# The tiles of an attention's close in a pool opened first: a two-layer graph attention kernel

## The chip, the cores and the metric

The kernel runs on one core of a Trainium2 chip. The metric is the device time of one execution in microseconds (us). A core has five engines, each with its own instruction stream in a fixed order: TensorE (PE in the profile; its weight loads are PEld), VectorE (DVE), ScalarE (ACT), GpSimd (POOL) and SyncE (SP), which here issues most of the DMAs. They wait for one another through semaphores.

## The reference, cut to what matters

4096 rows of 256 numbers go through three graph attentions with four heads each, an iterated feed-forward net (FFN) after the first, and a routed mixture of experts (MoE) after the third:

```python
def gat(x, adj, W, a):                       # 4 heads, D = 64
    h = einsum('nf,hfd->hnd', x, W)
    e = leaky_relu(f1[:, :, None] + f2[:, None, :], 0.2)   # f1, f2: h against a
    att = softmax(where(adj > 0, e, NEG))
    return elu(einsum('hnm,hmd->hnd', att, h))

x = x + gat(layernorm(x), adj, L0)           # first attention
x = x + ffn(layernorm(x))                    # 30 steps
h1 = gat(layernorm(x), adj, W1, a1)          # second attention
x = x + gat(h1, adj, W2, a2)                 # third attention
x = x + moe(layernorm(x))                    # top 2 of 6 experts
```

The third attention takes all its rows from the second one's result.

## The kernel before, in words

The function `attention` is called three times, with tags g0, g1 and g2. Each call has two stages.

**Preparation.** The 4096 rows are taken in eight groups of 512. For a group, `load` brings its rows into one of four slots of the tile `ring`, `columns` transposes them on PE (L114, into the PSUM tile `tp`) and ACT copies them to `xT` (L276). `products` multiplies by the weights (PE, L302, into two PSUM tiles `ph`), DVE copies the score columns out to `fs` (L320), ACT the rest to `hc` (L322). In the first group `greatest` finds a maximum (L283 to L292). Then come the exponentials `bd` (L329), the row `rt` that is stored to memory as `fd`, the scaled values `v` (L370) and, by `upper` and `lower`, the split tile `vals` (L377, L382), 66,560 bytes of each partition. `vals` stays for the second stage.

**Main loop.** 128 units follow one another, one for each of four chunks of 1024 rows, four heads and eight steps of 512 columns. ACT and DVE form a step mask `st` from the broadcast scores `f1b` (L461, L459), DVE joins it with the adjacency mask `m` (L567) and makes its complement `below` (L573), PE multiplies both by `vals` into the PSUM tile `acc` (L519). The order of DVE and ACT is written out by hand here; elsewhere a planner sets the order of each engine's stream, and it takes the waits for memory into account.

**The close.** When the eight steps of a chunk and head are done, ACT takes `lo` from `acc` (L468), DVE adds to `u` (L472) and works on `u` in five more operations (L482 to L494), ACT takes an exponential `e` (L497), and `finish` combines them (L623 or L625, then L626) and stores `e` (L627): to `h1d` in the second attention, and in the third to `x3d`, after adding the tile `old` that was loaded from `x2d`. A close is spread over the next unit's steps. Only the last one of an attention has nothing to hide behind.

The tiles of the on-chip memory come from pools. A pool takes the next free bytes when it is opened, in the manner of a stack, and gives them back when its scope ends; a tile that is put over an older one waits for everything that still reads or writes the older one. Within `attention` the pools were opened in this order: `lay` (r, nf2, hs), `vals`, `mask`, `f`, `steps`; then, for the preparation alone, `prep` and `pw` (xs, fs, mb, xT, hc, gm, bd, rt, v), which are closed at its end; and then `end` (u, lo, z, e, and old) and `work` (below). So `end` and `work` lie where the preparation had been, and since the three calls have the same pools, the third call's preparation lies where the second call's `end` is.

After the third attention the MoE opens its own pools from the same place on: bT, acc (32 KB, the running result), the expert weights ew0 to ew2, then the router's tiles. Its function `route` normalises rows (DVE L101 to L111, POOL's power L106, DVE L1108 and L1111), transposes (PE L1119), multiplies twice (L1098, ACT's relu L1100, L1128), and sorts rows to experts; POOL makes index constants (L1043 to L1072); SP loads the experts' weights (L1296). The main loop over tiles of 128 gathered rows follows (gather L1312, weight copies L1343).

Of the kernel before, what the change touches and what calls it, by code (L numbers as in the profile page):

```python
# [46 lines left out]
def gnn_ffn_kernel(ctx: ExitStack, tc: tile.TileContext, a: dict, out: bass.AP):  # L47
# [113 lines left out]
    def attention(tag, src, norm, w, front, chunks, first, ends, following, side={}):  # L161
# [7 lines left out]
        with ExitStack() as scope:  # L169
            lay = scope.enter_context(tc.tile_pool(name=f"{tag}_lay", bufs=1))  # L170
            r = lay.tile([P, NT, H], F32, name="r")
            nf2 = lay.tile([P, NT, H], F32, name="nf2")
            hs = lay.tile([P, 1, H, DV], F32, name="hs")
            vals = scope.enter_context(tc.tile_pool(name=f"{tag}_vals", bufs=1)).tile(
                [P, NT, H, 2, 2, DV], F16, name="vals"
            )
# [258 lines left out]
                )  # L435
                nc.gpsimd.memset(hs[:, 0, :, D : D + 1], TINY * N)  # L436

            end = scope.enter_context(tc.tile_pool(name=f"{tag}_end", bufs=1))
            if first:
                mask.append(scope.enter_context(tc.tile_pool(name=f"{tag}_mask1", bufs=4)))  # L440
            work = scope.enter_context(tc.tile_pool(name=f"{tag}_work", bufs=2))
            ps_o = scope.enter_context(tc.tile_pool(name=f"{tag}_pso", bufs=1, space=PSUM))
# [294 lines left out]
    first = ctx.enter_context(tc.tile_pool(name="f_first", bufs=4))  # L737
# [49 lines left out]
    def front(prep, small_ps):  # L787
# [22 lines left out]
        1: [(measure, 3), (init, 0), (init, 1), (rate, 2), (rate, 3)],  # L810
    }
    attention(
        "g0",
        x,
# [183 lines left out]
    for n in range(2):  # L998
        attention(
            f"g{n + 1}",  # L1000
            h1d if n else x2d,
            not n,
            layers[n + 1][0],
            None if n else centre_weights,
            [8, 8, 8, 8],
            False,
            to_rows(x3d, x2d) if n else to_rows(h1d),
            [NG // 2, x3d, runs_of] if n else [2, h1d],
            {} if n else side,
        )  # L1010
# [7 lines left out]
    with ExitStack() as scope:  # L1018
# [261 lines left out]
        with tc.tile_pool(name="r_ps", bufs=1, space=PSUM) as psum, tc.tile_pool(  # L1280
            name="r_pst", bufs=4, space=PSUM
# [186 lines left out]
```

## Time and profile before

| what | us |
|---|---|
| median of 3 runs | 2985.34 |
| lowest and highest | 2984.63, 2988.94 |
| the profiled execution | 2984.29 |
| its span, first to last instruction | 2982.6 |
| last `acc` matmul of the second attention ends | 2111.2 |
| first `below` of the third attention | 2178.72 |
| last `acc` matmul of the third attention ends | 2661.4 |
| first gather of the MoE | 2712.5 |

The page gives busy times, the granted clock of PE and the groups of instructions; the timeline gives single instructions with their start in us from the start of the span, their duration, and in brackets the time that the engine had been idle before and what released it. All times in this document from one kernel's trace are of one execution.

### The profile page before, as it was taken

To read this page: it belongs to the slowest core of one execution; us is meant where nothing else is said; L and a number is where in the kernel's file an instruction comes from. 1 tells how busy PE (TensorE), PEld (TensorE's weight loads), DVE (VectorE), ACT (ScalarE), POOL (GpSimd) and SP (SyncE) were. 2 spreads that over 40 slices of the span, in tenths; PEclk is the share of its full clock that TensorE was granted. 3 is DMA by queue.
4 is the path that set the end of the run, shared out by engine and by line. 5 is a ranking of instruction groups with operands and counts; after the bars stand their busy time and mean duration, and the time that the engine had idled before them with its cause. 6 is when DMAs were issued, how large, how long until landed. Compare 5 with 4: busy or idle time off the path is not lost. (4 is left out here: it accounts for less than half of the span.)

```text
span 2982.6 us, 82658 instructions
## 1 busy us (share of the span) xinstructions
PE 2801.3 (94%) x33923; PEld 2561.3 (86%) x33923; DVE 2740.8 (92%) x5769; ACT 2465.6 (83%) x3125; POOL 1153.7 (39%) x1084
## 2 busy tenths in 40 slices
PE   7899999979999999999998999999889999986996
PEld 5899999958888888888887999999789999975996
DVE  7999999999999999999998899999689999986775
ACT  6799999888888888888877999999699999963342
POOL 3000000079999999999982000000200000014663
PEclk9999999989999999999999999999999999998998
DMA  9999885153333333333353022120302132123253
GB/s 288 274 256 250 224 248 140 27 128 68 68 68 68 68 68 68 68 68 68 68 115 111 27 97 74 47 87 27 107 20 94 52 108 80 52 90 133 80 173 135
DMA packets 484450, 320.07 MB, mean 107 GB/s; under 512 B 416589, under 2 KB 445418, under 8 KB 477930
## 3 DMA queue, kind: packets, MB, share of 16 engines
q1 hardware_dynamic: 474034, 290.27, 36.7%
q0 software_dynamic: 7104, 19.41, 2.1%
q8 instruction: 268, 4.39, 0.6%
q10 hardware_dynamic: 2936, 5.11, 0.5%
q14 instruction: 108, 0.88, 0.1%
HBM read 183.00 MB, written 52.04 MB: 79 GB/s over the span
## 5 line engine op out<-in xcount | busy, mean ns | idle before, releaser
L519 PE MATMUL acc<-vals,st 128*128 128x130 f16 x12288 | 1430.7, 218 | 37.7 <-DVE u L472 30.2
L519 PE MATMUL acc<-vals,below 128*128 128x130 f16 x12288 | 1430.3, 221 | 12.9 <-DVE below L573 12.2
L461 ACT ACTIVATE st<-f1b,nf 128x1024 int8<-128x1024 f32 x1265 | 1334.5, 1140 | 30.8 <-PE acc L519 23.0
L519 PEld LDWEIGHTS <-below 128*128 128x128 fp8e4 x12288 | 1175.0, 96 | 53.4 <-issue 46.8
L519 PEld LDWEIGHTS <-st 128*128 128x128 fp8e4 x12288 | 1207.1, 98 | 8.9 <-DVE st L567 7.0
L935 PE MATMUL po<-wT,zT 128*128 128x256 f32 x1920 | 575.4, 382 | 6.9 <-ACT zT L922 3.7
L938 PE MATMUL po<-w,zT 128*128 128x256 f16 x3840 | 577.3, 273 | 0.4 <-DMA zT<-z 0.4
L906 POOL TENSOR_TENSOR th<-th,y 128x1024 f32<-128x1024 f32 x232 | 548.6, 2365 | 14.8 <-DVE z_st L915 0.4
L938 PEld LDWEIGHTS <-zT 128*128 128x128 f16 x3840 | 375.8, 98 | 161.3 <-DMA zT<-z 1.1
L573 DVE TENSOR_TENSOR below<-m,st 128x1024 int32<-128x1024 int32 x384 | 469.9, 1224 | 32.6 <-DVE st L567 0.9
L567 DVE TENSOR_TENSOR st<-st,m 128x1024 int32<-128x1024 int32 x384 | 467.1, 1216 | 0.2
L875 DVE SCALAR_TENSOR_TENSOR y<-po,z_rs,bias 128x256 f32<-128x256 f32 x928 | 384.3, 476 | 2.2 <-PE tp L867 0.7
L915 DVE BATCH_NORM_STATS2 z_st<-z 128x6 f32<-128x256 f32 x960 | 335.4, 411 | 0.0
L935 PEld LDWEIGHTS po<-wT,zT 128*128 128x128 f32 x1920 | 290.9, 192 | 16.4 <-ACT zT L922 4.5
L891 ACT ACTIVATE z<-th 128x1024 f32<-128x1024 f32 x240 | 251.8, 1049 | 17.4 <-POOL th L906 16.7
L106 POOL TENSOR_TENSOR ln_rstd<-ln_rstd,mhalf 128x4 f32<-128x4 f32 x24 | 31.0, 1293 | 578.0 <-ACT acc L1121 491.7
L926 POOL TENSOR_TENSOR z_rs<-z_rs,mhalf 128x4 f32<-128x4 f32 x240 | 245.0, 1021 | 3.1 <-ACT z_rs L925 3.1
L905 ACT ACTIVATE th<-y 128x1024 f32<-128x1024 f32 x232 | 241.9, 1043 | 0.0
L922 ACT COPY zT<-tp 128x512 f32<-128x512 f32 x240 | 140.2, 584 | 91.0 <-PE tp L867 89.8
L459 DVE TENSOR_SCALAR st<-f1b,nf 128x1024 int8<-128x1024 f32 x271 | 201.0, 742 | 7.5 <-PE acc L519 7.5
L758 POOL TENSOR_TENSOR x_rs<-x_rs,mhalf 128x4 f32<-128x4 f32 x8 | 9.4, 1174 | 501.8 <-ACT x_rs L757 501.8
L436 POOL MEMSET hs<- 128x4 f32 x3 | 0.3, 101 | 492.5 <-DVE u L489 492.5
(263 smaller groups left out, 3133.6 us busy)
## 6 DMA issues: line engine op xcount, KB each, us to landing
ring<-in_adj_dram SPq DMA_DIRECT2D x64, 1024.0 KB
m<-edges SPq DMA_DIRECT2D x32, 1024.0 KB
f1b<-fd SPq DMA_DIRECT2D x48, 512.0 KB
edges<-m SPq DMA_DIRECT2D x16, 1024.0 KB
y<-yd SPq DMA_DIRECT2D x16, 512.0 KB
ew<-in_L_ffn_expert_w_dram SPq DMA_DIRECT2D x18, 256.0 KB
t<-in_x_dram SPq DMA_DIRECT2D x8, 512.0 KB
old<-in_x_dram SPq DMA_DIRECT2D x16, 256.0 KB
```

Source lines behind the costliest of these rows:

```text
L461: nc.scalar.activation(out, f1, AF.Sign, bias=f2, scale=-1.0)
L519: nc.tensor.matmul(acc[:, i, cols], masked[part][:, at_i // TR, s, rows], v[:, cols], start=(j == 0 and part == 0), stop=(j == NT - 1 and ...
L567: nc.vector.tensor_tensor(above, above, whole, OP.bitwise_and)
L573: nc.vector.tensor_tensor(below, whole, above, OP.bitwise_xor)
L875: nc.vector.scalar_tensor_tensor(t[:, r, :] if end else y[:, g * G + r, :], po[:, r, :], rstd[:, r : r + 1], t[:, r, :] if end else bias, ...
L891: ins = nc.scalar.activation(z, th.pop(u), AF.Silu, scale=0.01)
L905: nc.scalar.activation(th[at], was, AF.Tanh, scale=0.01)
L906: ins = (nc.gpsimd if at else nc.vector).tensor_tensor(th[at], th[at], was, OP.add)
L915: nc.vector.bn_stats(st[:, r, :], z[:, r, :])
L926: nc.gpsimd.tensor_tensor(rs[u], rs[u], mhalf, OP.pow)
L935: nc.tensor.matmul(po[:, r, :], src[:, r * P : (r + 1) * P], wT, start=True, stop=False)
L938: nc.tensor.matmul(po[:, r, :], src16[:, part * G + r, :], w16[:, other, :], start=False, stop=(part == 1 and other == 1),)
```

## The change

In the second and third attention the pool `end` is opened right after `lay`, ahead of `vals`; it is no longer opened after the preparation. In the first attention it stays where it was. No operation is added or removed.

```diff
             hs = lay.tile([P, 1, H, DV], F32, name="hs")
+            end = None if first else scope.enter_context(tc.tile_pool(name=f"{tag}_end", bufs=1))
             vals = scope.enter_context(tc.tile_pool(name=f"{tag}_vals", bufs=1)).tile(
                 [P, NT, H, 2, 2, DV], F16, name="vals"
             )
...
-            end = scope.enter_context(tc.tile_pool(name=f"{tag}_end", bufs=1))
             if first:
+                end = scope.enter_context(tc.tile_pool(name=f"{tag}_end", bufs=1))
                 mask.append(scope.enter_context(tc.tile_pool(name=f"{tag}_mask1", bufs=4)))
             work = scope.enter_context(tc.tile_pool(name=f"{tag}_work", bufs=2))
```

From the added line on, the line numbers of the kernel after are one higher than here (L303 for L302, and so on).

## The prediction

> **What bounds the kernel now.** I read the page first for which engine sets the pace, then the timeline around the place where the second attention ends and the third is prepared, then the one-microsecond stretches there with TensorE's granted clock, and last the timeline where the third attention ends, since the same pool lies under the router's tiles.
>
> ```profile
> PE 2801.3 (94%) x33923; PEld 2561.3 (86%) x33923; DVE 2740.8 (92%) x5769; ACT 2465.6 (83%) x3125; POOL 1153.7 (39%) x1084
> ```
>
> TensorE (PE) is busy 94% of the span, so time is to be had only where it stands still. The page's chain of work that ended last begins at 2633 us and doesn't reach the seam at 2111 us. The timeline there (start, duration, engine, line, form, then idle time before it and its releaser), first PE, then VectorE (DVE), ScalarE (ACT) and the DMA queue of SyncE (SP):
>
> ```profile
> 2112.61 1.09 PE L114 MATMUL tp<-ident,ring 128*128 128x128 f32 x8 [1.43 <-DVE u L472]
> 2122.43 5.99 PE L302 MATMUL ph<-g_w,xT 128*128 128x264 f32 x16 [8.73 <-ACT xT L276]
> ...
> 2116.88 0.69 DVE L626 SCALAR_TENSOR_TENSOR e<-e,u 128x512 f32<-128x512 f32 x1
> 2126.36 0.17 DVE L320 COPY fs<-ph 128x16 f32<-128x16 f32 x1 [8.79 <-PE ph L302]
> 2128.45 0.17 DVE L320 COPY fs<-ph 128x16 f32<-128x16 f32 x1 [1.92 <-PE ph L302]
> ...
> 2115.75 0.63 ACT L497 ACTIVATE e<-u 128x512 f32<-128x512 f32 x1 [3.93 <-DVE u L494]
> 2121.69 0.60 ACT L276 ACTIVATE xT<-tp 128x512 f32<-128x512 f32 x1 [5.31 <-DMA h1d<-e]
> ...
> 2117.60 0.37 SPq L627 DMA_DIRECT2D h1d<-e  x1
> ```
>
> The third attention's first rows are loaded and transposed by 2113.70. Their copy into xT nevertheless starts at 2121.69, released by the landing of the close's last store, 4.09 us after its issue. PE stands for 8.73 us. That isn't a need of the data: rows 0 to 511 have nothing to do with the last chunk's result. It is the memory. In the built program the close's tiles (u, lo, z, e) lie at bytes 171104 to 181536 of each partition, and xT's two buffers at 173376 to 181568.
>
> The clock column (PE, its weight loads, DVE, ACT, POOL busy; then the clock) for four of these microseconds:
>
> ```profile
> 2114.00:2115.00 1.00, 0.00 (x0) 0.00 (x0) 0.92 (x3) 0.00 (x0) 0.10 (x1) 1.00 0.95 401
> 2116.00:2117.00 1.00, 0.00 (x0) 0.00 (x0) 0.55 (x2) 0.38 (x1) 0.00 (x0) 0.80 1.03 437
> 2124.00:2125.00 1.00, 1.00 (x4) 0.80 (x3) 0.00 (x0) 0.00 (x0) 0.00 (x0) 0.50 0.00 0
> 2127.00:2128.00 1.00, 1.00 (x6) 0.87 (x5) 0.00 (x0) 0.15 (x1) 0.00 (x0) 1.00 0.00 0
> ```
>
> The standstill costs twice: at 2116.8 the clock falls to half, and the 16 matmuls that follow take 5.99 us, where the same 16 take 3.83 later (2155.81).
>
> [...] 0.50 from 2117, 1.00 again 4 us into the matmuls. [...] reusing e's bytes costs the store's 4.09 us and not its 0.37 us of issue. [...] in the trace, DVE slows beside POOL's work there: four scalings L1111 took 1.38 us at 2669.67 and 2.14 at 2680.20 beside POOL's casts.
>
> **The change part by part.** It adds and removes no instruction, byte or load; it moves tiles. In the second and third attention the close's tiles go to 47200 to 57632, under vals. The preparation then starts at 181536, where the below tiles lie (181536 to 193824).
>
> 1. Start of the second attention: vals and the masks move 10,432 bytes up over other FFN tiles. Wait for wait, its instructions wait for the same ones as before. Cost 0; were the cover gone, PE's last FFN matmul would already hold the same tiles.
>
> 2. Seam from second to third, the gain. The first xT now waits only for the transposes and DVE's last sum; ACT takes both halves ahead of e. Step by step: transposes end 2113.70; xT 2113.73 to 2114.99 (two halves took 1.26 us at 2121.69), so e at 2115.75 isn't delayed. PE starts 0.74 us after xT's start, as before: 2114.47. It then has stood 0.77 us, so I take the warm 3.83 us: the second ph ends at 2118.3. DVE is now the one to be late: in its order the close still stands ahead of fs, until 2117.57. So the first fs is at 2117.6 (its ph, five eighths of the matmuls in, is there at 2116.9) and the second at 2118.35, against 2128.45: **10.1 us less**. With a cold clock (5.99 us) the second ph ends at 2120.46: 8.0 us less. I take warm: the clock held for 5.6 us after the last attention matmul (2111.2), and now new matmuls come after 3.3. What follows is one chain (maximum, mb, bd, v, vals), which moves along: from 2131 to 2178 us ACT is busy 43.7 and DVE 41.7 of 47 us, and both move as one, so nothing there takes the gain up. External times that don't move: the next-layer masks fill the DMA queues until 2120, first used at 2152.89; the row load of group 4 was issued at 2113.73 and is needed near 2130; groups 6 and 7 read the last chunk, landed 2121.69, and their load would come at 2122.5, after it. On SP's queue the last store stands between the loads of groups 4 and 5; its time is unchanged and group 5's slot frees at about 2119.5. Cost 0 each.
>
> 3. Entry to the router, where three waits change:
>
> ```profile
> 2666.74 1.04 POOL L106 TENSOR_TENSOR ln_rstd<-ln_rstd,mhalf 128x4 f32<-128x4 f32 x1 [491.71 <-ACT acc L1121]
> 2673.91 0.21 POOL L1043 IOTA along_i<- 128x37 int32 x1
> 2678.53 1.05 POOL L106 TENSOR_TENSOR ln_rstd<-ln_rstd,mhalf 128x4 f32<-128x4 f32 x1
> ...
> 2665.54 2.42 SPq L1296 DMA_DIRECT2D ew<-in_L_ffn_expert_w_dram  x5
> 2669.04 0.37 SPq L627 DMA_DIRECT2D x3d<-e  x1
> ...
> 2690.00:2695.00 5.00, 0.00 (x0) 0.00 (x0) 4.20 (x19) 0.93 (x3) 0.00 (x0) 0.85 1.01 402
> 2695.00:2700.00 5.00, 0.38 (x4) 0.16 (x3) 4.27 (x21) 0.61 (x1) 0.00 (x0) 0.50 0.07 28
> ```
>
> POOL's constants needed the close's bytes; now they need only the last matmuls (2661.3) and are ordered ahead of the first power L106. They hold it for about 6.6 us (2673.91 to 2681.55 less one power of 1.05), to 2667.9 instead of 2666.74; its user on DVE, nmr, came at 2669.22 and hides that, but casts beside the close's two-input sums may add up to 1.5. The fourth power, queued behind the constants until 2678.53, is free at about 2677. The router's acc now lies over e (45248 to 78016), and bT, which the first relu needs, also waits for the last x3d store: issued 2669.04, landing at 2673.1 by the 4.09 us above. bT stands in DVE's order ahead of the second n, which so starts up to 1.2 us late; three acc of 1.07 us on ACT stand before the first relu, which comes at 2676.4 to 2677.1 instead of 2676.22. PE is nearly full from 2670.13 to 2689.95 and follows: logits done between 0.1 earlier and 0.5 later. The five expert loads ahead of that store now come after it: all 18 (256 KB each) start at about 2673.5 instead of 2665.5. At the 400 GB/s of these rows 4.7 MB take 12 us, so they land near 2692 with the others between them, ahead of the first use at 2700.7. Unseen in the trace is how the constants run beside the close: bounds 2 us gained (fourth power) and 2.5 lost (first power, bT, relu in a row). I take **0.5 us lost**.
>
> Sum: -10.1 + 0.5 = -9.6 us. The profiled execution took 2984.29 us (span 2982.6), so 2974.7; the median of the three runs, 2985.34, lies 1.05 above it, so I say **2975.7**.
>
> **The rivals.** *Cold clock.* The transposes may not count as activity[...]. Against it: clock 1.00 up to 2116. Gives -8.0 + 0.5: 2977.8. *The router gains*: -10.1 - 2.0 gives 2973.2; for it speaks nmr at 2679.61, which waited for that fourth power, against it that PE is full there. *No change*: another wait at the seam takes over, so that xT or ph still comes with the close's store. The wait lists speak against it; 2985.3. *Slower*: the expert loads, pushed behind the store, land late, and the loop's first weight copies (2700.7 on ACT) wait. Each microsecond past 2700.7 costs one; from 2710.3 on the gain is eaten, which needs 4.7 MB in 37 us, 128 GB/s instead of 400. At 100 GB/s they'd land at 2720.5: 19.8 lost, 2995.5.
>
> **How the numbers follow.** Forecast 0.66, cold clock 0.15, router gains 0.10, no change 0.05, slower 0.04. The range runs from 2972.0 (router's bound of 2 and 1.2 of run-to-run spread) to 2980.5 (cold clock, router's loss of 2.5, and 0.7 of spread). 0.2%, 6 us, is about what a measurement of this kernel can tell from no change; cold clock with the worst router gives only -5.5 and counts as no change. Faster 0.88, same 0.08, slower 0.04.
>
> **What would show it.** Right: ACT's first xT of the third attention near 2114 with PE tp as releaser, the matmuls L302 after under 1 us of idle time in about 3.8 us, fs following e within 1 us, the third attention's first below 10 us earlier. Step 3 right: the stretch from the last acc matmul to the first gather, 51.1 us now (2661.4 to 2712.5), within 2.5 of that. Wrong: PE idle over 3 us before L302, or w<-ew released by a DMA.

## The result, and the profile after

The kernel after takes 2977.12 us (median of 7 runs, 2973.72 to 2981.28), the kernel before, also in 7 runs, 2987.28 us (2982.51 to 2988.94): a ratio of 0.9971, 95% interval 0.9962 to 0.998. That is 8.7 us less by the ratio, between 6.0 and 11.4. Run again later, where both took 11 to 13 us longer, the same two kernels stood at 0.9956 [0.9942, 0.9969], 13.2 us less. The profiled execution after took 2978.01 us, its span 2976.1, against 2982.6 before. The page's first row after:

```profile
PE 2800.0 (94%) x33923; PEld 2562.3 (86%) x33923; DVE 2740.5 (92%) x5769; ACT 2465.1 (83%) x3125; POOL 1157.6 (39%) x1084
```

PE is busy 1.3 us less, DVE and ACT as long as before: the time came out of standstills, and of the matmuls that ran at half clock.

The seam from the second to the third attention, timeline of the kernel after, PE first, then DVE, ACT and SP's queue:

```profile
2113.65 1.09 PE L114 MATMUL tp<-ident,ring 128*128 128x128 f32 x8 [1.43 <-DVE u L473]
2115.52 3.83 PE L303 MATMUL ph<-g_w,xT 128*128 128x264 f32 x16 [0.78 <-ACT xT L277]
...
2117.93 0.69 DVE L627 SCALAR_TENSOR_TENSOR e<-e,u 128x512 f32<-128x512 f32 x1
2118.53 0.17 DVE L321 COPY fs<-ph 128x16 f32<-128x16 f32 x1
2119.39 0.18 DVE L321 COPY fs<-ph 128x16 f32<-128x16 f32 x1 [0.69 <-PE ph L303]
...
2114.78 0.60 ACT L277 ACTIVATE xT<-tp 128x512 f32<-128x512 f32 x1 [1.92 <-PE tp L114]
2116.80 0.63 ACT L498 ACTIVATE e<-u 128x512 f32<-128x512 f32 x1 [0.75 <-DVE u L495]
...
2118.65 0.37 SPq L628 DMA_DIRECT2D h1d<-e  x1
```

Read from the transposes' start (2113.65), since executions of one and the same kernel reach this place up to 2.4 us apart. ACT takes xT 1.13 us after it, released by the transposes and no longer by the store, which is issued only 3.9 us later. PE stands 0.78 us instead of 8.73, and its 16 matmuls take 3.83 us instead of 5.99. The second fs comes 5.74 us after the transposes' start; before it was 15.84. This is 10.1 us less. DVE's tail of the close now ends last: the first fs follows e<-e,u without a gap.

The entry to the router, first one line of DVE in the kernel before, then the timeline of the kernel after (POOL, DVE, SP's queue, ACT, POOL):

```profile
2663.10 0.68 DVE L482 TENSOR_TENSOR u<-u,r 128x520 f32<-128x520 f32 x1
...
2652.68 0.17 POOL L1044 IOTA along_i<- 128x37 int32 x1 [486.60 <-PE acc L520]
2660.40 1.47 POOL L106 TENSOR_TENSOR ln_rstd<-ln_rstd,mhalf 128x4 f32<-128x4 f32 x1
...
2654.24 1.05 DVE L483 TENSOR_TENSOR u<-u,r 128x520 f32<-128x520 f32 x1
2661.91 0.16 DVE L1109 SCALAR_TENSOR_TENSOR nmr<-ln_mv,ln_rstd 128x4 f32<-128x4 f32 x1 [0.77 <-POOL ln_rstd L106]
2662.39 1.38 DVE L1112 TENSOR_SCALAR n<-ring,ln_rstd,nmr 128x256 f32<-128x256 f32 x4
...
2667.46 11.04 SPq L1297 DMA_DIRECT2D ew<-in_L_ffn_expert_w_dram  x16
...
2692.53 1.66 ACT L1344 COPY w<-ew 128x512 f32 x3 [6.16 <-DMA ring<-x3d]
...
2704.31 1.61 POOL L1313 DMA_INDIRECT gx<-nd,source  x1 [0.25 <-DVE ln_mv L103]
```

POOL runs the index constants from 2652.68 on, beside the close, and gets to its first power only at 2660.40; nmr waits for it. I measure from the start of the last close's u<-u,r, which the constants hardly move (from the second lo of the close, ahead of it, the loss is 0.68). In the kernel before it was at 2663.10: the first scaled n came 6.57 us later (2669.67) and the first gather 49.41 (2712.51). After, these are 8.15 and 50.07. The router lost 0.66 us.

In the two profiles of the kernel after, these stretches agree within 0.3 us while the spans differ by 16 (2976.1 and 2992.2). The table gives them from each profile (us): from the third attention's first transposes to the second fs, to the attention's last u<-u,r, from there to the first gather, and the sum of the last two.

| kernel | to fs | to u<-u,r | to gather | sum |
|---|---|---|---|---|
| before | 15.84 | 550.49 | 49.41 | 599.90 |
| after | 5.74 | 540.59 | 50.07 | 590.66 |
| after, run again | 5.74 | 540.83 | 50.10 | 590.93 |
| pool early for the second only | 5.74 | 537.71 | 49.42 | 587.13 |
| pool early for the third only | 5.73 | 539.94 | 50.17 | 590.11 |
| only e early | 12.15 | 547.00 | 51.04 | 598.04 |
| before, with fillers | 13.61 | 548.27 | 49.41 | 597.68 |
| after, constants ahead | 5.73 | 540.31 | 48.93 | 589.24 |
| second only, constants ahead | 5.74 | 537.76 | 48.68 | 586.44 |
| after, late expert loads | 5.73 | 540.55 | 51.95 | 592.50 |

So 599.90 less 590.66, 9.2 us, is what the change is worth in these stretches. The rest of an execution, the start up to the transposes and the expert loop after the first gather, spreads: the loop took 270.1 us in the profile before (2712.5 to 2982.6), 271.8 after, and 279.9 to 285.4 in the later runs; in the kernel after itself it was then 285.3.

### The profile page after: what moved, and what is told of

It reads as the page before. It is cut to its first block, busy times and chain, and to the rows that moved or that the text cites. A ratio compares the mean times of both kernels' runs of the same rounds, so it can differ in the third digit from the quotient of the medians.

```text
span 2976.1 us, 82659 instructions
## 1 busy us (share of the span) xinstructions
PE 2800.0 (94%) x33923; PEld 2562.3 (86%) x33923; DVE 2740.5 (92%) x5769; ACT 2465.1 (83%) x3125; POOL 1157.6 (39%) x1084
```

## The experiments

**The pool early for the second attention only.** This takes the gain and the loss apart.

```diff
-            end = None if first else scope.enter_context(tc.tile_pool(name=f"{tag}_end", bufs=1))
+            end = None if tag != "g1" else scope.enter_context(tc.tile_pool(name=f"{tag}_end", bufs=1))
...
-            if first:
+            if end is None:
                 end = scope.enter_context(tc.tile_pool(name=f"{tag}_end", bufs=1))
+            if first:
```

> The kernel after, with the early pool for the second attention only; the third attention's close keeps its tiles in the late pool. Theory (the gain comes from the seam alone, the router loses 0.7 us by its constants running ahead): at the seam as after, xT released by PE's transposes, 16 ph matmuls in 3.83 us, the second fs 7.1 us after the last attention matmul (before 17.2, after 7.1); at the router as before: the constants after the first power, the sums and e of the close at 0.68 us each, and 51.0 us from the second lo of the close to the first gather (before 50.99, after 51.67). Total 0.7 us below the kernel after. Rival A (the router's part is noise): the stretch is 51.67 or more here too. Rival B (the gain needs both attentions' pools moved): the second fs comes 17 us after the last matmul.

2985.24 us, 0.9954 [0.9939, 0.9969] of before. The timeline at both places (PE at the seam; POOL, then DVE, at the router):

```profile
2113.68 3.83 PE L303 MATMUL ph<-g_w,xT 128*128 128x264 f32 x16 [0.78 <-ACT xT L277]
...
2653.16 1.04 POOL L106 TENSOR_TENSOR ln_rstd<-ln_rstd,mhalf 128x4 f32<-128x4 f32 x1 [490.75 <-ACT acc L1123]
2660.32 0.22 POOL L1045 IOTA along_i<- 128x37 int32 x1
...
2649.52 0.68 DVE L484 TENSOR_TENSOR u<-u,r 128x520 f32<-128x520 f32 x1
```

The seam is as after and the router as before: the power stands ahead of the constants, and the gather comes 49.42 us after u<-u,r. The seam's gain and the router's loss are thus two separate effects: the first needs only the second attention's tiles moved, the second comes from the third's.

Neither the theory nor its rivals had a third effect: from the transposes to u<-u,r it takes 537.71 us, 2.9 less than after. The planner put the third attention's preparation in another order on ACT and DVE. In the kernel after, ACT makes the first masks st ahead of the fourth group's hc (st, vals, st, vals, hc), and PE, whose next ph tile needs that hc, stands 2.39 us ahead of 2140.34. In the other order the masks come one group later, and the longest such wait is 1.71 us. By the first below 2.0 us of the difference are there (56.23 after the transposes against 54.22). That the order is the cause is argued from the traces, not shown: no run changed the order alone.

**The pool early for the third attention only.** The mirror image of it (`tag != "g2"` in the same line).

> Early pool for the third attention only: the second's close keeps its tiles at 171104 to 181536, and it is the third's preparation that moves, up to 181536. Theory (what counts is that xT doesn't lie over the close's tiles, whichever of the two moves): xT released by PE's transposes, second fs 5.74 us after the transposes' start, as after; at the router the constants ahead of the first power as after, u<-u,r to the first gather 50.1. Its preparation of the third attention stands in another order on ScalarE, nearer to that of the pool for the second alone: transposes to u<-u,r between 537.7 and 540.6. Rival (the second's pool must move): second fs 15.84 us after the transposes' start.

2988.36 us, 0.9959 [0.9943, 0.9974]. xT was released by the transposes, the second fs came 5.73 us after their start, and the router lost what it had lost after (50.17). So moving either side is enough at the seam: with the second's tiles left at 171104, the third's xT stands above 181536. What decides is that the two don't share bytes. The way to u<-u,r took 539.94 us, between the two. Here too ACT takes the fourth group's hc ahead of the first mask, and PE's longest wait for hc is 1.28 us, yet only 0.65 of the 2.9 us are gained. So the long wait alone isn't what costs them; which part of the order does, or whether it is the order at all, stays open.

**Only e in an early pool.** u, lo and z of the close stay under xT.

```diff
+            epool = None if first else scope.enter_context(tc.tile_pool(name=f"{tag}_e", bufs=1))
...
-                e = end.tile([P, CM, D], F32, name="e")
+                e = (epool or end).tile([P, CM, D], F32, name="e")
```

> The kernel before, with only the tile e of the close in an early pool of its own (second and third attention); u, lo and z stay below the third's preparation. xT then waits for the last VectorE operation that reads u (e<-e,u, 0.69 us) instead of the landing of the store of e. Theory (the 10.1 us are three terms: 4.1 us of landing, 3.9 of order behind the close's tail, 2.1 of clock): xT starts about 6.4 us after the last attention matmul's end (before 10.5), released by DVE; ph has stood 4.6 us and still runs at the lower clock, near 6 us for 16 matmuls (3.83 if the clock has not fallen yet); the second fs 13.1 us after the last attention matmul (before 17.2, after 7.1), so 4.1 us gained, or 6.2 with the clock up. Rival (the store's landing is all of the cost): the second fs at 7 us, 10 us gained.

2996.64 us, 0.9992 [0.9983, 1.0001]. The timeline at the seam (PE, ACT, DVE):

```profile
2119.57 6.30 PE L303 MATMUL ph<-g_w,xT 128*128 128x264 f32 x16 [4.72 <-ACT xT L277]
...
2118.83 0.60 ACT L277 ACTIVATE xT<-tp 128x512 f32<-128x512 f32 x1 [1.30 <-DVE e L627]
...
2125.91 0.17 DVE L321 COPY fs<-ph 128x16 f32<-128x16 f32 x1 [2.24 <-PE ph L303]
```

xT now waits for DVE's last operation on u instead of the landing. The second fs comes 12.15 us after the transposes (2113.76): 3.7 of the 10.1 us gained. The rival, that the landing is all of it, falls. After the standstill of 4.72 us the clock stands at 0.50 (2118 to 2124), and here that costs a little more (6.30 us for the 16) than it did after 8.73 (5.99). The router lost 1.6 us besides: its constants wait for the close's e and so land between the first and the second power, beside the scaled n, whose first two groups of four take 2.03 and 2.16 us instead of 1.38.

**The store's wait kept, the clock held up.** The kernel before, with matmuls of a constant in the standstill.

```diff
+FILL = 32
...
+                    if g == 0 and not norm:
+                        filler = ps_m.tile([P, C], F32, name="filler")
+                        for _ in range(FILL):
+                            nc.tensor.matmul(filler[:, :P], mean, mean, start=True, stop=True)
```

> The kernel before, with 32 matmuls 128x128 of a constant tile on TensorE between the third attention's first transposes and its first ph matmuls; the close's tiles stay where they were and xT still waits for the landing of the store. Theory (the lower clock after the standstill is 2.1 us of the 10.1): the fillers run from about 2113.7 to 2118 at the full clock, xT still starts 10.5 us after the last attention matmul, released by the DMA h1d<-e, and the 16 ph matmuls take about 3.8 us instead of 5.99: the second fs 15.1 us after the last attention matmul instead of 17.2, 2.1 us gained. Rival (the 5.99 us are of the matmuls' own start, not of the clock): 5.99 us again and nothing gained.

2997.13 us, 0.9995 [0.9986, 1.0004]. The timeline (PE, ACT):

```profile
2112.86 7.31 PE L415 MATMUL filler<-mean 128*128 128x128 f32 x64
2121.67 3.83 PE L303 MATMUL ph<-g_w,xT 128*128 128x264 f32 x16 [1.50 <-ACT xT L277]
...
2120.93 0.60 ACT L277 ACTIVATE xT<-tp 128x512 f32<-128x512 f32 x1 [5.23 <-DMA h1d<-e]
```

The fillers ran 7.31 us, longer than I had thought (64 in the trace). xT still came 9.00 us after the transposes' start (2111.93), as in the kernel before (9.08), but the clock stayed at 1.00 (2112 to 2127) and the 16 ph took 3.83 us. The second fs came at 13.61 instead of 15.84: 2.2 us are the clock. The rival falls.

**The index constants ahead of the second attention.** The kernel after; along, along16, place, code, before, before16, all16 and order are made in the pool `late`, right after `layer(2, ...)` is set up.

```diff
-    layer(2, ctx.enter_context(tc.tile_pool(name="late", bufs=1)))
+    late = ctx.enter_context(tc.tile_pool(name="late", bufs=1))
+    layer(2, late)
+    along = numbers("along", [(1, max(T, NH // P))], 0, 0)
...
+    order = late.tile([P, NTH, E], F32, name="order")
```

> The kernel after, with the router's index constants on GpSimd made ahead of the second attention, so that at the router GpSimd has only the powers of the layer norm. Theory (the 0.7 us lost at the router is these constants, which hold the first power and slow VectorE's sums of the close from 0.68 to 1.05 us): the first power starts within 0.5 us of its input, the sums take 0.68 us, the first scaled n starts about 1.6 us earlier than after relative to the second lo of the close (8.15 us instead of 9.75), and from that lo to the first gather 50.0 to 51.0 us (after 51.67). Rival (TensorE or VectorE holds the router, the constants are covered): the first n earlier, but the first gather as after, 51.5 us or more. Elsewhere as after, and the making of the constants at the earlier place costs nothing, or up to 8 us if GpSimd's masks are late there.

2989.78 us, 0.9969 [0.9958, 0.9979]. The timeline at the router (POOL, DVE, POOL):

```profile
2658.43 1.59 POOL L106 TENSOR_TENSOR ln_rstd<-ln_rstd,mhalf 128x4 f32<-128x4 f32 x1 [491.12 <-DVE ln_rstd L105]
...
2655.48 0.68 DVE L483 TENSOR_TENSOR u<-u,r 128x520 f32<-128x520 f32 x1
...
2704.41 1.61 POOL L1315 DMA_INDIRECT gx<-nd,source  x1 [0.25 <-DVE ln_mv L103]
```

The power follows its input at once, u<-u,r takes 0.68 us instead of 1.05, the first n comes 6.47 us after it (after: 8.15) and the gather 48.93 (after: 50.07). So where the change had let them run, the constants cost the kernel after 1.1 us, and the rival, that they are covered, falls. Of a first n that is 1.7 us earlier, 0.5 is covered further on. The third attention is as after (540.31). Made ahead of the second attention, the constants show no cost there: from the FFN's last matmul to the second attention's first below it took 64.13 us, in the kernel before 64.08 and after 63.54. The total doesn't show the gain, only the stretch does.

**The best version.** The pool early for the second attention only, and the constants ahead.

> Early pool for the second attention only, and the router's index constants made ahead of the second attention: the two versions that were ahead of the kernel after, put together. Theory: transposes to u<-u,r 537.7 us as with the pool for the second alone (its preparation stands in the same order), u<-u,r to the first gather 48.9 to 49.4 us; 3.5 to 4 us below the kernel after. Rival (the 2.9 us in the third attention were not of that order): 540.6 and 49, about 1 us below the kernel after.

2985.22 us against 2988.36 of the kernel after on the same chip, and 0.9953 [0.9939, 0.9966] of before. By the stretches it is 4.2 to 4.5 us below the kernel after (586.44 against 590.66 and 590.93), so both parts are there. The total time can't show it: the interval of the kernel after, 0.9942 to 0.9969, overlaps.

> The kernel after itself, beside the others on the same chip. Theory: the same landmarks as in its first profile, so that the differences to the first runs' kernels are of the kernels: from the third attention's first transposes to the second fs 5.74 us, to the first below 56.2, to the close's last u<-u,r 540.6, from there to the router's first gather 50.1. Rival (the shorter third attention of the kernel with the early pool for the second alone, 537.7, was that chip or that run): 537.7 here too.

The kernel after beside it took 2988.36 us, with the stretches of its first profile within 0.3 us, so the shorter third attention above is not that of a run or a chip.

**Late expert loads.** The prediction's slower rival, priced.

```diff
+LATE = 18
...
+            spare = dram.tile([LATE, GR // 2, C], F32, name="spare")
+            for i in range(LATE):
+                nc.sync.dma_start(spare[i], x3d[N - GR // 2 :, :])
             for i in range(3):
                 src = a[f"L1_ffn_expert_w{i + 1}"]
```

> The kernel after with 18 more copies in DRAM (256 KB each, of the last rows of x3d into a spare tile) on SP's queue ahead of the expert loads; they compute nothing. It prices the prediction's slower rival, expert loads that come too late. Theory (they had about 10 us of slack after): 4.7 MB, read and written, delay the expert loads by 12 us if copies move at 400 GB/s and by 24 if at 200; the first w<-ew, about 0.5 us after pos in the kernel after, then waits for a DMA by 2 to 14 us, and what is behind the loads on SP's queue, the rows of x3d and of n, comes later too, so the first gather shifts by a like amount: 2 to 14 us slower than the kernel after. Rival (the loads have much more slack than that, or the copies go beside them): no change.

2994.39 us, 0.9982 [0.9973, 0.999], against 2988.36 of the kernel after on the same chip. The timeline (SP's queue, ACT, DVE, PE):

```profile
2676.98 13.42 SPq L1301 DMA_DIRECT2D ew<-in_L_ffn_expert_w_dram  x18
...
2692.33 1.66 ACT L1348 COPY w<-ew 128x512 f32 x3 [6.15 <-DMA ew<-in_L_ffn_expert_w_dram]
...
2711.89 0.16 DVE L1110 SCALAR_TENSOR_TENSOR nmr<-ln_mv,ln_rstd 128x4 f32<-128x4 f32 x1 [5.28 <-POOL ln_rstd L107]
...
2712.77 2.07 PE L1356 MATMUL ph<-xT,w 128*128 128x128 f32 x8 [3.18 <-DVE xT L1330]
```

From u<-u,r (2652.59) the loads are issued 14 us later than after. Yet w<-ew starts 0.90 us after pos does (2691.43), as in the kernel after: the loads that it needs have that much slack, although the row now names them. The theory, that w<-ew would wait by 2 to 14 us, fails in this. What comes too late are the rows for the router's second half, which are issued behind the loads on SP's queue (ring<-x3d at 2693.09, 13.6 us later from u<-u,r than after). Their statistics and nmr then stand in DVE's order ahead of the first experts' xT, and nmr waits 5.28 us for POOL's power. The gather comes 1.9 us later, and the first expert matmul 60.2 us after u<-u,r instead of 56.2. The added copies also let the planner change the router's order, so these 3.9 us are not the transfers' alone.

## Why the prediction was right, point by point

**Forecast and total.** 2975.7 was said and 2977.12 measured, within the range of 2972.0 to 2980.5. That these lie so near is in part luck: the time before that the forecast started from, 2985.34, is 1.9 us below the later median of 7. Against its own time before, the sum was -9.6; the stretches give -9.2, the ratio -8.7 with 6.0 and 11.4 as ends. The two profiled spans differ by only 6.5, because the start (1.05) and the expert loop (1.7) of that execution were longer. They can't be read as effects of the change: the two profiles of the kernel after differ by 2.4 and 13.4 us there.

**Step 1, start of the second attention, cost 0.** Right. From the second attention's first below to the third's first transposes 485.45 us before (from 1627.16), 485.70 after (from 1627.95; 486.19 when run again), 485.31 with the second only. Of the later start, 0.8 us lies ahead of the second attention.

**Step 2, the seam, 10.1.** Right in each number. From the transposes' start the prediction had xT at 1.12, ph at 1.86, the two fs at 4.99 and 5.74 us; measured 1.13, 1.87, 4.88 and 5.74. The clock stayed at full speed (3.83 us for the 16), as was chosen over the cold rival, but the reason given wasn't shown. The prediction took it that the clock holds for 5.6 us after the last attention matmul; in the kernel before it fell at 2116.60, at an edge of a grid of 3.41 us on which all its changes in that trace lie (last section). An estimate from the trace after: a stretch of that grid that began as the last attention matmul ended (2112.22, 1.4 us ahead of the transposes) would have held only 1.2 us of work, a share of 0.35, and in the kernel before the clock fell after a stretch of that share (2171.21 to 2174.63, PE busy for 1.19 us). In the two profiles of the kernel after, a stretch began 2.6 and 2.1 us ahead of the transposes. So this term came out right with some luck. The split is now measured: 3.7 us by taking e's bytes out (landing), 6.4 more by letting xT go ahead of the close's tail, and 2.2 to 2.5 of the total are the clock (2.2 with fillers; 6.30 less 3.83 at the end of the first two). The step's claim that what follows moves along held: at the first below 9.9 us of the gain are left (66.11 against 56.23), and 9.9 at the end of the attention.

The external times were right too, but the phrase that nothing there takes the gain up hid something. The third attention after the seam isn't an immovable chain: the version with the second pool alone, in which the planner ordered the same instructions otherwise, took 2.9 us less for it, and the cause stays open.

**Step 3, the router, 0.5 lost.** Measured 0.66; right in direction, place and nearly in size. The term that was mis-sized is the first power. The constants were to hold it for about 6.6 us; they took 7.72 (2652.68 to 2660.40), beside the close's sums: 1.1 more, where the prediction had allowed up to 1.5, an estimate of the author. From u<-u,r the power came 6.16 us later instead of 3.64: 2.5 us late, near the far end of the 1.2 and up to 1.5 more. The cover that I named, nmr's own lateness, took this down to 1.6 us at the first n, and the nearly full PE behind it to the rest. The fourth power was to come 1.5 earlier and came 1.0 earlier (14.42 us after u<-u,r instead of 15.43). bT delayed the second n by at most 0.3 us beyond the first, not 1.2. The first relu came 1.3 us later (14.45 us after u<-u,r instead of 13.12), past the 0.2 to 0.9 that was said, and the last logits 0.66 later, past the 0.5. The expert loads went behind the store as said and cost nothing. The row of w<-ew does name a DMA, the sign that was set for being wrong; but w<-ew starts 0.90 us after pos does, in the kernel before 0.86 with pos as releaser, so no load held it.

**The rivals.** The cold clock, another wait at the seam, and late loads didn't occur. That the router gains is wrong for this change, but the bound of 2 us gained wasn't empty: constants made elsewhere gain 0.5 us against before. The point from which late loads decide, 2710.3, was argued for w<-ew; the run with added copies shows that the rows behind the loads on the queue cost time before w<-ew waits at all.

## What to carry to other kernels

Where an engine waits at a seam between stages for a store that its data don't need, look at which tiles share bytes: here moving either one was enough (second fs at 5.74 and 5.73 us instead of 15.84), and the wait for the landing (3.7 us) also brought the order of the writer's tail (6.4 more); 2.2 to 2.5 us of the sum were TensorE's clock. Then ask what the moved bytes had been holding back: here a batch of constants that had been kept late by its memory ran early and stood in front of a short chain. With a planner, every change of memory can also change the order elsewhere, so compare stretches between landmarks before a cause is given to a total.

## What was not expected of the hardware

A standstill of TensorE of nearly one length dropped the clock in one execution and not in another. In the third attention's preparation PE stood 2.39 us in the kernel after and 2.47 us in the second profile of the same kernel. First the kernel after, then the second profile, each with PE's timeline and with stretches of 3.41 us in the columns of the prediction (behind the window its length, then PE busy; the clock is third from the end):

```profile
2140.34 5.51 PE L303 MATMUL ph<-g_w,xT 128*128 128x264 f32 x16 [2.39 <-ACT hc L323]
2138.32:2141.73 3.41, 1.39 (x6) 1.23 (x7) 3.41 (x6) 3.41 (x9) 0.62 (x1) 1.00 0.00 0
...
2142.78 3.83 PE L303 MATMUL ph<-g_w,xT 128*128 128x264 f32 x16 [2.47 <-ACT hc L323]
2137.80:2141.21 3.41, 2.52 (x16) 1.88 (x14) 3.10 (x4) 3.08 (x4) 1.28 (x2) 1.00 0.31 105
2141.21:2144.62 3.41, 1.84 (x8) 1.61 (x9) 3.41 (x6) 3.41 (x10) 1.07 (x1) 1.00 0.00 0
```

The two differ in where the standstill falls on a grid. In each of the traces before and after, all changes of the clock lie whole multiples of 3.4133 us apart, within 0.01 us, and the grid lies differently in the two (from 2116.60 in the one to 2141.73 in the other it is 7.36 such stretches). In the kernel after, the clock fell at 2141.73, at the end of a stretch in which PE had been busy for 0.41 of the time: 1.39 us of work in it didn't hold the clock. In the second profile an edge cut the standstill in two, and the stretches on both sides, at a clock of 1.00, were busy for 0.74 and 0.54. From 2090 to 2200 us in the traces before and after, the five stretches at full clock that ended in a drop were busy for 0.15 to 0.42, and all others for 0.55 or more; the clock came back after five stretches that were busy throughout, and stayed down after six with 0.41 or less. Elsewhere in these two traces the border is less sharp: drops are found up to 0.64 and stretches that kept the full clock down to 0.42. That the busy share sets the clock is thus not shown; near the seam the two went together.

The half clock from 2141.73 on cost nothing further on: the first below came 56.23 us after the transposes' start, in the second profile 56.21.

At the seam all seven profiles with xT ahead of the store kept the full clock: the second fs came 5.73 or 5.74 us after the transposes' start, and the 16 ph took 3.83 us in the six whose timelines show them whole. In the kernel after, the two stretches there were busy for 0.58 and 0.77 (from 2111.01 and 2114.42), in its second profile the one with the transposes for 0.52 (2113.90 to 2117.32, 1.79 us). That speaks for the transposes' counting as work there, which the prediction's cold rival had doubted: an estimate from these numbers, without their 1.09 us, is 0.20, and the clock fell after shares of 0.15 to 0.42.

Where POOL's constants ran beside the close, it was not always the same engine that was slowed. u<-u,r (DVE) took 1.05 us instead of 0.68; of the two casts beside it, one of 512 columns took 0.61 as elsewhere and the next, into before, 0.77 instead of 0.35. Then a cast of 512 columns took 1.16 beside u<-u,hs at 0.66.
